# The softmax of a cross-attention on VectorE alone: maximum and sum over the partitions by 32x32 transposes and moves between quadrants

## The chip, the core and the metric

The kernel runs on one core of a Trainium2 chip. The metric is the device time of one execution in microseconds (us). Engines: TensorE (PE) for matrix products, its weight loads listed apart as PEld; VectorE (DVE); ScalarE (ACT); GpSimd (POOL); SyncE (SP), which here only issues transfers.

## What is computed

Everything is float32. `x` has 16 batches of 128 tokens of width 512, `ctx` has 16 batches of 2048 rows of width 512. The reference runs three blocks in order, each on a layer norm of `x`, each added to `x`:

```python
# 1. cross-attention, no projections
scores = einsum('bld,bvd->blv', layernorm(x), ctx)      # 16 x 128 x 2048
x = x + einsum('blv,bvd->bld', softmax(scores, -1), ctx)
# 2. causal self-attention, 16 heads of 32, through 64-wide latents, rotary
#    positions on half of each head
x = x + attention(layernorm(x)) @ Wc
# 3. a mixture of 8 experts of rank 64, two chosen for a batch by its first token
x = x + ffn(layernorm(x))
```

The change lies in the softmax of the first block.

## The kernel before

The program is written out for all 16 batches and three generators are stepped by hand: `score(b)` and `attend(b)` for the cross-attention, `inner(b)` for the self-attention, `experts(b)` for the third block. One pass of the main loop works on four batches at a time: the self-attention of batch b, the rest of the cross-attention (`attend`) of b + 1, the scores of b + 2, and the first norm of b + 3; the experts are those of b - 1.

`score(b)` keeps the scores **transposed**: 128 rows of `ctx` on the partitions, the 128 tokens along the free dimension, so that the exponentials can serve as weights of the next product without being turned. `sc` holds four quarters `v` of [128, 4, 128]. A softmax over the context is then a maximum and a sum over four quarters, over four groups, and over the 128 partitions. Before the change this goes as follows.

- For each quarter TensorE writes `psc`, ACT copies it to `sc`, DVE keeps the running maximum `mx`. `halved` folds four groups to one with two instructions of DVE.
- Over the partitions: TensorE transposes the 128x128 maxima (`tr_m`), DVE reduces each row (`nm`), multiplies the identity with it (`diag`), and TensorE multiplies a matrix of ones with `diag`, which leaves the negated maximum of every token on all partitions (`spread`, in PSUM).
- DVE adds `spread` to the four quarters, ACT takes the exponentials.
- DVE adds the four quarters (`sums`), folds them (`fold`, `last_fold`) to `part`, and in `attend` TensorE multiplies `part` with a column of ones (`den`). DVE takes the reciprocal `rden`, and one instruction, `x<-av,rden,x`, divides and adds the residual.

In the loop these pieces are spread out. The order on TensorE in one pass is: `psc` of b + 2 (with `mid` of the experts inside), `ffn`, `y` of b, `v` of b + 1, `tr_m`, `o` of b, `spread`, then in the next pass `k`, `q`, the first quarter of `av`, the scores of the self-attention (`pss_sc`, `pss_acc`), three more quarters of `av`, `den`, the logits `lg` of the experts, and `psc` again.

Around the change in the same pass, on DVE: the residual of the self-attention (`x<-o,x` of line 687), the norm for the experts (`norm_pieces`: statistics, aggregate, a root on POOL, then `h`), its block transpose (`blocks`, line 268), which SP sends through DRAM to get a full transpose, and the rotary positions for k and q (`rotated`, `turned`): a shuffle, a product with the sines on POOL, a product with the cosines on DVE, and their sum. ACT then makes `kb` out of `kT`. The shuffled k and the shuffled q use one buffer, the tag "partner" with one copy (line 555).

**What sets the order.** Transfers and all of TensorE's instructions are kept in the order in which they are traced. On the other engines a scheduler orders what has no pin, by what it reckons to be ready, and by the order of tracing among those. A pin

```python
def pinned(ins):
    if not closing:
        tc.keep_in_program_order(ins)
```

puts one instruction behind whatever was traced just before it on the same engine, and says nothing about what may come between. In `inner` the shuffles, the cosines and the sums `kT`, `qT` are pinned. The loads of `ctx` and `ctxT` are issued by ACT's queue (`queue = nc.scalar`, line 1049), and `load` pins them too. The end of the last passes is ordered by hand (`CLOSING`). PSUM has three pools: `ps_tr` with 3 banks (`tr_m`, `spread`, `den`, `lg`), `ps_sc` with 2, and `ps_acc` with 3 (`k`, `q`, `av`, `pss_acc`, `mid`, `ffn`, `y`, `v`, `o` in turn).

Of the kernel before, what the change touches and what calls it, by code (L numbers as in the profile page):

```python
# [11 lines left out]
F32 = mybir.dt.float32  # L12
I32 = mybir.dt.int32
U32 = mybir.dt.uint32
AF = mybir.ActivationFunctionType
ALU = mybir.AluOpType
AX = mybir.AxisListType
PSUM = bass.MemoryType.PSUM

P = 128  # L20
B, S, V, D = 16, 128, 2048, 512
# [4 lines left out]
VC = V // 512  # L26
# [4 lines left out]
QD = P // 4  # L31
# [58 lines left out]
def perceiver_block(ctx: ExitStack, tc: tile.TileContext, io: dict, out: bass.AP):  # L90
# [3 lines left out]
    p1 = ctx.enter_context(tc.tile_pool(name="p1", bufs=1))  # L94
    p2 = ctx.enter_context(tc.tile_pool(name="p2", bufs=2))
# [26 lines left out]
    vector, scalar, gpsimd = InOrder(nc.vector), InOrder(nc.scalar), InOrder(nc.gpsimd)  # L122
# [13 lines left out]
    def matmul(*args, **kwargs):  # L136
        tc.keep_in_program_order(nc.tensor.matmul(*args, **kwargs))  # L137
# [11 lines left out]
# [3 lines that stand above are left out]
# [18 lines left out]
    def bank(pool, tag, name):  # L170
        return pool.tile([P, 512], F32, tag=tag, name=name)
# [35 lines left out]
    def layernorm(src, name, mix=False):  # L207
        h, pieces = norm_pieces(src, name, mix=mix)
        for piece in pieces:
            ins = piece()  # L210

            if ins is not None and name.startswith("1_") and piece is not pieces[1]:
                pinned(ins)
        return h
# [46 lines left out]
    def transposed(src, dst, name, by_tensor):  # L261
        n = src.shape[1] // P
        if by_tensor:
            for piece in tensor_pieces(lambda: src, dst, name, n):
                piece()
        else:
            blocks = p1.tile([P, 4, n, QD], F32, tag=f"blocks_{name[0]}", name=f"blocks_{name}")
            vector.transpose(blocks, src.rearrange("p (n q i) -> p q n i", n=n, q=4))
            ways[name] = blocks, dst
# [4 lines left out]
    def named(b, **of):  # L274
        for name, piece in of.items():
            pieces[f"{name}.{b}"] = piece
# [53 lines left out]
    scores, firsts, values, lasts, routes = {}, {}, {}, {}, {}  # L330
# [24 lines left out]
    def first_norm(x, hT):  # L355

        stats = const.tile([P, 6], F32, name="st_first")
        mv, rstd = const.tile([P, 2], F32, name="mv_first"), const.tile([P, 1], F32, name="rs_first")
        vector.bn_stats(stats, x)
        vector.bn_aggr(mv, stats)  # L360
        pinned(gpsimd.tensor_scalar_add(rstd, mv[:, 1:2], EPS))
        gpsimd.tensor_tensor(rstd, rstd, mhalf, ALU.pow)
        h = p2.tile([P, D], F32, tag="h", name="h_1_0")
        for c in range(KC):

            tr = bank(ps_tr, "tr", f"tr_1_0_{c}") if c else bank(ps_acc, "acc", "tr_1_0_0")
            at = slice(c * P, (c + 1) * P)
            vector.tensor_scalar(
                mixed(h)[:, c], plain(x)[:, c], mv[:, 0:1], rstd, ALU.subtract, ALU.mult
            )  # L370
            transpose(tr[:, :P], h[:, at], ident)
            scalar.copy(hT[:, :, c, :], tr[:, :P].rearrange("p (a j) -> p a j", a=4))
            warm_up(1)


    def score(b):

        hT = p1.tile([P, 4, KC, QD], F32, tag="hT1" if b != 1 else "hT3", name=f"hT1_{b}")
        if b:
            h = layernorm(xs[b], f"1_{b}", mix=b == 1)  # L380
            yield
            transposed(h[:], hT, f"1_{b}", b == 1)
        else:
            first_norm(xs[b], hT)
            yield
        yield

        sc = p2.tile([P, VC, 4, S], F32, tag="sc", name=f"sc_{b}")
        mx = p1.tile([P, 4, S], F32, tag="mx", name=f"mx_{b}")
        for v, ct in enumerate(turned_cts.pop(b)):  # L390
            ps = bank(ps_sc, "sc", f"psc_{b}_{v}").rearrange("p (j t) -> p j t", j=4)
            for j in range(4):

                if v == VC - 1 and j == 3:
                    yield
                for c in range(KC):
                    matmul(
                        ps[:, j, :].rearrange("p (a i) -> p a i", a=4),
                        ct[:, c, j * P : (j + 1) * P], hT[:, :, c, :],
                        start=(c == 0), stop=(c == KC - 1),  # L400
                    )
            scalar.copy(sc[:, v], ps)

            if v:
                vector.tensor_tensor(mx, ps, mx if v > 1 else sc[:, 0], ALU.max)
            if v < VC - 1:
                yield

        def halved(t, op):
            vector.tensor_tensor(t[:, :2], t[:, :2], t[:, 2:], op)  # L410
            vector.tensor_tensor(t[:, 0], t[:, 0], t[:, 1], op)
            return t[:, 0]

        most = halved(mx, ALU.max)
        yield

        tr = bank(ps_tr, "tr", f"tr_m_{b}")
        transpose(tr[:, :S], most, ident)
        nm = p2.tile([P, 1], F32, tag="nm", name=f"nm_{b}")
        vector.tensor_reduce(nm, tr[:, :S], AX.X, ALU.max, negate=True)  # L420
        diag = p1.tile([P, S], F32, tag="diag", name=f"diag_{b}")
        vector.tensor_scalar(diag, ident, nm, None, ALU.mult)
        yield
        spread = bank(ps_tr, "tr", f"spread_{b}")
        matmul(spread[:, :S], ones, diag, start=True, stop=True)
        for v in range(VC):
            vector.tensor_tensor(
                sc[:, v], sc[:, v], spread[:, None, :S].to_broadcast([P, 4, S]), ALU.add
            )
            scalar.activation(sc[:, v], sc[:, v], AF.Exp)  # L430
        part = p2.tile([P, S], F32, tag="part", name=f"part_{b}")
        scores[b] = (sc, part)
        yield
        sums = p1.tile([P, 4, S], F32, tag="sums", name=f"sums_{b}")
        pinned(vector.tensor_tensor(sums, sc[:, 0], sc[:, 1], ALU.add))
        yield
        for v in range(2, VC):
            pinned(vector.tensor_tensor(sums, sums, sc[:, v], ALU.add))

        def fold():  # L440
            vector.tensor_tensor(sums[:, :2], sums[:, :2], sums[:, 2:], ALU.add)

        def last_fold():
            vector.tensor_tensor(part, sums[:, 0], sums[:, 1], ALU.add)

        if b == B - 1:
            named(b, fold=fold, last_fold=last_fold)
        else:
            fold()
            last_fold()  # L450
        yield

    def attend(b):

        sc, part = scores.pop(b)
        acc = bank(ps_acc, "acc", f"av_{b}")
        ct = cts.pop(b)

        def quarter(v):
            for j in range(4):  # L460
                matmul(
                    acc, sc[:, v, j, :], ct[v][:, j, :],
                    start=(v == 0 and j == 0), stop=(v == VC - 1 and j == 3),
                )

        state = {}

        def whole():
            den = state["den"] = bank(ps_tr, "tr", f"den_{b}")
            matmul(den[:, :1], part, ones[:, :1], start=True, stop=True)  # L470

        rden = Later(p2, [P, 1], tag="rden", name=f"rden_{b}")

        def inverse():
            vector.reciprocal(rden[:], state["den"][:, :1])

        x1 = Later(p2, [P, D], tag="x1", name=f"x1_{b}")

        def added():
            vector.scalar_tensor_tensor(x1[:], acc, rden[:], xs.pop(b), ALU.mult, ALU.add)  # L480

        if b == B - 1:
            quarter(0)
            named(
                b, av1=lambda: quarter(1), av2=lambda: quarter(2), av3=lambda: quarter(3),
                den=whole, rden=inverse, x1=added,
            )
            h, norm = norm_pieces(x1, f"2_{b}", mix=True)
            named(b, **dict(zip(("st2", "mv2", "rs2", "h2"), norm)))
            firsts[b] = x1, h  # L490
            yield
            return
        for v in range(VC):
            quarter(v)
            if v == (VC - 1 if b else VC - 2):
                whole()
                inverse()
            if v < VC - 1:
                yield
        added()  # L500
        firsts[b] = (x1, layernorm(x1, f"2_{b}", mix=b == 0))
        yield
# [487 lines left out]
    def warm_up(n):  # L990
        for _ in range(n):
            matmul(warm[:, :P], ones, ones, start=True, stop=True)
# [166 lines left out]
```

## Time and profile before

| what | value |
|---|---|
| median of 3 runs | 810.46 us (810.45 to 811.42) |
| profiled execution: its own time | 810.97 us |
| its span in the profile | 809.2 us |
| granted TensorE clock | 0.998 |
| PE busy | 800.2 us (99%) |
| DVE busy | 529.7 us (65%) |
| ACT busy | 260.4 us (32%) |
| POOL busy | 146.6 us (18%) |
| moved by DMA | 211.05 MB, 261 GB/s on average |

Busy times are sums of the durations of an engine's instructions. A group of instructions is given as line, engine, operation, `out<-in`, shape and count; its line is often that of a helper (L137 is the wrapper of every matmul, L115 that of every instruction of DVE, ACT and POOL), so groups are told apart by their tiles. In a timeline the first number is the start from the span's beginning, the second the length of the merged piece, both in us; a bracket at the end gives the idle time before it and what ended it.

### The profile page before, as it was taken

The numbers are of one execution on the slowest core, as the hardware profiler recorded it, in microseconds if no ns is written. First come the engines' busy times: TensorE is split into PE (matmuls) and PEld (weight loads), VectorE is DVE, ScalarE is ACT, GpSimd is POOL, SyncE is SP. The second block draws the span as 40 slices with busy tenths as digits, with TensorE's granted clock in tenths as the row PEclk, the third lists the DMA queues.
The fourth block names the chain that finished last, engine by engine and source line by source line (L and its number), as shares of the span: only waits on it lengthen the run. The fifth ranks groups of instructions, "written<-read, shape, count | busy, mean of one in ns | idle before, by whom it ended". The sixth has DMA issues, their size and how long they took to land.

```text
span 809.2 us, 14363 instructions
## 1 busy us (share of the span) xinstructions
PE 800.2 (99%) x5538; PEld 568.5 (70%) x5538; DVE 529.7 (65%) x1234; ACT 260.4 (32%) x772; POOL 146.6 (18%) x213
## 2 busy tenths in 40 slices
PE   9999999999999999999999999999999999999996
PEld 9946775768677576866758677676867757686653
DVE  2455759386684947658495775938667584856885
ACT  2232324142232423233241232415223241422461
POOL 1001011212121121211112121111212112121204
PEclk9999999999999999999999999999999999999999
DMA  9998394967849497694958859495885949664102
GB/s 375 417 389 321 118 380 171 340 253 251 360 163 381 172 324 292 221 397 142 364 212 292 320 188 399 152 353 222 281 337 181 388 152 340 261 231 173 41 1 79
DMA packets 76868, 211.05 MB, mean 261 GB/s; under 512 B 6400, under 2 KB 42624, under 8 KB 60416
## 3 DMA queue, kind: packets, MB, share of 16 engines
q10 hardware_dynamic: 15696, 113.32, 35.0%
q1 hardware_dynamic: 57168, 84.75, 29.4%
q0 software_dynamic: 3936, 12.07, 4.4%
q8 instruction: 44, 0.72, 0.3%
q14 instruction: 24, 0.20, 0.1%
HBM read 180.23 MB, written 29.88 MB: 260 GB/s over the span
## 4 chain that ended last, share of the span: by engine, by line
PE 97%; DVE 1%; POOL 0%; issue 0%; ACT 0%; POOLq 0%
PE psc L137 28%; PE av L137 28%; PE k L137 7%; PE q L137 7%; PE v L137 7%; PE o L137 6%; PE pss_sc L137 2%; PE y L137 2%; PE ffn L137 2%; PE pss_acc L137 2%; PE mid L137 2%; PE warm L137 1%; PE tr_m L140 0%; PE tr L140 0%; PE spread L137 0%; PE lg L137 0%
## 5 line engine op out<-in xcount | busy, mean ns | idle before, releaser
L137 PE MATMUL psc<-hT,ctxT 128*128 128x128 f32 x2048 | 235.0, 276 | 0.0
L137 PEld LDWEIGHTS psc<-hT,ctxT 128*128 128x128 f32 x2048 | 231.3, 192 | 0.5 <-issue 0.5
L137 PE MATMUL av<-ctx,sc 128*128 128x512 f32 x512 | 227.3, 596 | 0.0
L137 PEld LDWEIGHTS av<-ctx,sc 128*128 128x128 f32 x512 | 94.4, 190 | 110.5 <-issue 107.9
L115 ACT ACTIVATE att<-att,nmx 128x128 f32<-128x128 f32 x256 | 98.8, 388 | 84.9 <-DVE nmx L115 84.9
L115 POOL TENSOR_SCALAR rs<-mv 128x1 f32<-128x1 f32 x47 | 10.6, 225 | 431.0 <-DVE g_at L115 209.5
L115 ACT COPY sc<-psc 128x512 f32<-128x512 f32 x64 | 37.5, 586 | 140.0 <-PE psc L137 140.0
L115 ACT ACTIVATE sc<-sc 128x512 f32<-128x512 f32 x64 | 40.2, 630 | 90.9 <-DVE sc L115 90.4
L137 PE MATMUL k<-hT,w_k 128*128 128x128 f32 x512 | 60.1, 275 | 0.0
L137 PE MATMUL q<-hT,w_q 128*128 128x128 f32 x512 | 60.0, 275 | 0.0
L137 PEld LDWEIGHTS k<-hT,w_k 128*128 128x128 f32 x512 | 58.5, 192 | 1.5 <-issue 0.8
L137 PE MATMUL v<-w_v,hT 128*32 128x512 f32 x520 | 59.0, 593 | 0.0
L137 PEld LDWEIGHTS q<-hT,w_q 128*128 128x128 f32 x512 | 58.5, 192 | 0.0
L137 PE MATMUL o<-w_c,yT 128*128 128x512 f32 x128 | 57.8, 594 | 0.0
L115 DVE TENSOR_TENSOR mx<-psc,mx 128x512 f32<-128x512 f32 x32 | 21.6, 676 | 55.0 <-ACT sc L115 55.0
L115 ACT ACTIVATE kb<-kT,cst 128x512 f32<-128x512 f32 (+1 forms) x34 | 36.2, 1113 | 39.8 <-DVE kT L115 39.8
L115 DVE TENSOR_SCALAR h<-x,mv,rs 128x512 f32<-128x512 f32 x47 | 27.4, 583 | 31.9 <-POOL rs L115 31.9
L115 ACT ACTIVATION_READ_ACCUMULATOR att<-att,nmx 128x1 f32 x256 | 47.9, 187 | 0.0
L115 DVE TENSOR_TENSOR sc<-sc,spread 128x512 f32<-128x512 f32 x64 | 42.6, 671 | 3.3 <-PE spread L137 3.3
L115 DVE TENSOR_TENSOR att<-att,rsm 128x512 f32<-128x512 f32 x64 | 43.4, 678 | 0.8
L115 DVE TENSOR_REDUCE nmx<-att 128x4 f32<-128x512 f32 x64 | 41.8, 671 | 0.1
L137 PEld LDWEIGHTS o<-w_c,yT 128*128 128x128 f32 x128 | 23.9, 196 | 23.8 <-issue 23.0
(139 smaller groups left out, 851.1 us busy)
## 6 DMA issues: line engine op xcount, KB each, us to landing
ctx<-in_ctx_dram ACTq DMA_DIRECT2D x56, 1024.0 KB, 8.4
ctxT<-in_ctxT_dram ACTq DMA_DIRECT2D x52, 1024.0 KB, 10.5
there_p<-pX SPq DMA_DIRECT2D x28, 512.0 KB, 4.0
pT<-there_p SPq DMA_DIRECT2D x28, 512.0 KB, 4.5
ctxT<-in_ctxT_dram SPq DMA_DIRECT2D x12, 1024.0 KB, 8.9
there<-blocks SPq DMA_DIRECT2D x42, 256.0 KB, 3.3
hT<-there SPq DMA_DIRECT2D x42, 256.0 KB, 3.0
ctx<-in_ctx_dram SPq DMA_DIRECT2D x8, 1024.0 KB, 10.5
```

The lines of the kernel that those rows point to most:

```text
L115: ins = issue(*args, **kwargs)
L137: tc.keep_in_program_order(nc.tensor.matmul(*args, **kwargs))
```

## The change

For batches 2 to 15 the maximum over the partitions stays on DVE. A new helper `across` transposes the 128x128 tile in blocks of 32x32, reduces along the free dimension to four values a partition, moves three quadrants of 32 partitions beside the first, and reduces again: partition i of the first quadrant then holds the values of tokens i, 32 + i, 64 + i and 96 + i. For the maximum four more block transposes of a broadcast write the result into all four quadrants, as `spread` in SBUF. The four subtractions follow at once, behind the last scores, and the first two exponentials with them; the last two exponentials and the first of the `sums` are traced one step later (behind the loads of the next `ctxT`), the other two `sums` another step later. Batches 2 to 14 take the denominator by `across` as well, with a reciprocal and four moves, and `attend` finds it ready, without `den`. Batches 0 and 1 keep the old way, and batch 15 keeps the old denominator, its `sums` where they were.

```diff
+    def across(t, name, op, negate=False):
+        turned = p1.tile([P, 4, QD], F32, tag="diag", name=f"turned_{name}")
+        pinned(vector.transpose(turned.rearrange("p q i -> p (q i)"), t))
+        each = p2.tile([P, 4, 4], F32, tag="each_quadrant", name=f"each_quadrant_{name}")
+        pinned(vector.tensor_reduce(each[:, 0, :], turned, AX.X, op))
+        for a in range(1, 4):
+            pinned(vector.tensor_copy(each[:QD, a, :], each[a * QD : (a + 1) * QD, 0, :]))
+        whole = p2.tile([P, 4], F32, tag="whole", name=f"whole_{name}")
+        pinned(vector.tensor_reduce(
+            whole[:QD], each[:QD].rearrange("p a q -> p q a"), AX.X, op, negate=negate
+        ))
+        return whole[:QD]
...
         most = halved(mx, ALU.max)
+        if b > 1:
+            spread = p1.tile([P, 4, QD], F32, tag="spread", name=f"spread_{b}")
+            peak = across(most, f"m_{b}", ALU.max, negate=True)
+            for a in range(4):
+                pinned(vector.transpose(
+                    spread[a * QD : (a + 1) * QD], peak[:, :, None].to_broadcast([QD, 4, QD])
+                ))
+            for v in range(VC):
+                pinned(vector.tensor_tensor(
+                    sc[:, v], sc[:, v],
+                    spread.rearrange("p j i -> p (j i)")[:, None, :].to_broadcast([P, 4, S]), ALU.add,
+                ))
+                if v < 2:
+                    scalar.activation(sc[:, v], sc[:, v], AF.Exp)
+            yield
+            for v in range(2, VC):
+                pinned(scalar.activation(sc[:, v], sc[:, v], AF.Exp))
+            sums = p1.tile([P, 4, S], F32, tag="sums", name=f"sums_{b}")
+            if b == B - 1:
...
+            pinned(vector.tensor_tensor(sums, sc[:, 0], sc[:, 1], ALU.add))
+            yield
+            for v in range(2, VC):
+                pinned(vector.tensor_tensor(sums, sums, sc[:, v], ALU.add))
+            yield
+            whole = across(halved(sums, ALU.add), f"den_{b}", ALU.add)
+            vector.reciprocal(whole, whole)
+            rden = p2.tile([P, 1], F32, tag="rden", name=f"rden_{b}")
+            for a in range(4):
+                vector.tensor_copy(rden[a * QD : (a + 1) * QD], whole[:, a : a + 1])
+            scores[b] = (sc, rden)
+            yield
+            yield
+            return
         yield
 
         tr = bank(ps_tr, "tr", f"tr_m_{b}")
...
-        rden = Later(p2, [P, 1], tag="rden", name=f"rden_{b}")
+        known = 1 < b < B - 1
+        rden = part if known else Later(p2, [P, 1], tag="rden", name=f"rden_{b}")
...
-            if v == (VC - 1 if b else VC - 2):
+            if not known and v == (VC - 1 if b else VC - 2):
                 whole()
                 inverse()
```

More of the change, by code (lines that the diff above doesn't have):

```diff
@@ L414, in score @@
         most = halved(mx, ALU.max)
+        if b > 1:
[17 more added lines that the diff above has]
+            if b == B - 1:
+                part = p2.tile([P, S], F32, tag="part", name=f"part_{b}")
+                scores[b] = (sc, part)
+                yield
[4 more added lines that the diff above has]
+                    pinned(vector.tensor_tensor(sums, sums, sc[:, v], ALU.add))
+                named(
+                    b, fold=lambda: vector.tensor_tensor(sums[:, :2], sums[:, :2], sums[:, 2:], ALU.add),
+                    last_fold=lambda: vector.tensor_tensor(part, sums[:, 0], sums[:, 1], ALU.add),
+                )
+                yield
+                return
+            pinned(vector.tensor_tensor(sums, sc[:, 0], sc[:, 1], ALU.add))
+            yield
+            for v in range(2, VC):
+                pinned(vector.tensor_tensor(sums, sums, sc[:, v], ALU.add))
+            yield
+            whole = across(halved(sums, ALU.add), f"den_{b}", ALU.add)
[4 more added lines that the diff above has]
+            scores[b] = (sc, rden)
+            yield
+            yield
+            return
         yield
@@ L444, in last_fold @@
             vector.tensor_tensor(part, sums[:, 0], sums[:, 1], ALU.add)
[L446 to L450, printed above, removed]
+        fold()
+        last_fold()
         yield
```

## The prediction

> **What bounds the kernel now.** I read the page first: the busy rows, then the chain that ended last. Both say TensorE (PE).
>
> ```profile
> span 809.2 us, 14363 instructions
> PE 800.2 (99%) x5538; PEld 568.5 (70%) x5538; DVE 529.7 (65%) x1234; ACT 260.4 (32%) x772; POOL 146.6 (18%) x213
> ...
> PE 97%; DVE 1%; POOL 0%; issue 0%; ACT 0%; POOLq 0%
> ```
>
> PE has almost no idle time; VectorE (DVE) has a third of the span free. So only what leaves PE, or makes PE wait, can move the time. The groups show what the change takes from PE: `tr_m` (16 records of 322 ns), `spread` (32 of 276 ns), `den` (32 of 208 ns). [...]the price on PE is the distance between starts. The timeline of PE over one steady iteration gives it; the other iterations repeat these distances every 47.86 us.
>
> ```profile
> 394.18 3.62 PE L137 MATMUL v<-w_v,hT 128*32 128x512 f32 x32
> 397.72 0.33 PE L140 MATMUL tr_m<-ident,mx 128*128 128x128 f32 x1
> 397.89 3.60 PE L137 MATMUL o<-w_c,yT 128*128 128x512 f32 x8
> 401.32 0.39 PE L137 MATMUL spread<-diag,ones 128*128 128x128 f32 x2
> 401.55 3.74 PE L137 MATMUL k<-hT,w_k 128*128 128x128 f32 x32
> 405.12 3.74 PE L137 MATMUL q<-hT,w_q 128*128 128x128 f32 x32
> 408.69 3.60 PE L137 MATMUL av<-ctx,sc 128*128 128x512 f32 x8
> 412.22 1.13 PE L137 MATMUL pss_sc<-kb,qT 64*128 64x256 f32 x8
> ...
> 424.55 0.28 PE L137 MATMUL den<-ones,part 128*128 128x1 f32 x2
> 424.69 0.37 PE L137 MATMUL lg<-g_part,ones 128*128 128x8 f32 x2
> ```
>
> The reader sees that `tr_m` holds PE for 0.17 us (397.72 to 397.89), `spread` for 0.23, `den` for 0.14. Then the timeline of DVE over the same stretch, to see what could make PE wait once these are gone:
>
> ```profile
> 398.42 0.29 DVE L115 TENSOR_SCALAR diag<-ident,nm 128x128 f32<-128x128 f32 x1
> 401.53 0.69 DVE L115 TENSOR_TENSOR x<-o,x 128x512 f32<-128x512 f32 x1 [2.82 <-PE o L137]
> 402.13 0.68 DVE L115 TENSOR_TENSOR sc<-sc,spread 128x512 f32<-128x512 f32 x1
> ...
> 405.10 0.55 DVE L115 TENSOR_SCALAR h<-x,mv,rs 128x512 f32<-128x512 f32 x1 [0.43 <-POOL rs L115]
> 405.56 0.68 DVE L115 TENSOR_TENSOR sc<-sc,spread 128x512 f32<-128x512 f32 x1
> 406.17 0.01 DVE L115 LOAD_MASK_SELECT kP<-k  x1
> 406.17 0.73 DVE L115 STREAM_SHUFFLE kP<-k 128x512 f32<-128x512 f32 x1
> ...
> 408.29 0.69 DVE L115 TENSOR_TENSOR kT<-kT,kP 128x512 f32<-128x512 f32 x1 [0.20 <-POOL kP L115]
> ...
> 411.31 0.69 DVE L115 TENSOR_TENSOR qT<-qT,qP 128x512 f32<-128x512 f32 x1 [0.89 <-POOL qP L115]
> ```
>
> This is the reading that decides. `qT` ends at 412.00 and `pss_sc`, which reads it, starts at 412.22; where PE waits for DVE in the closing it starts 0.05 us after DVE's end (`h` 762.81, `tr` 762.86), so the slack is 0.17 us. And from the k shuffle on the chain is rigid: shuffle, POOL's product with the sines (1.28 us), `kT`, then the q shuffle, which must wait because `kP` and `qP` share one buffer ("partner"), POOL again, `qT`. From shuffle k (406.17) to the end of `qT` it takes 5.83 us. Shuffle k itself was late because of DVE: k was through on PE at 405.12, and 0.21 us later DVE could have had it (the distance at 72.08 to 72.29, where DVE did wait for k); but it was busy until 406.17. So whatever DVE does between `x<-o,x` (called x2 below) and shuffle k already sits 0.17 us under the critical path.
>
> **The change part by part.**
>
> *Removed from PE*, for batches 2 to 15 `tr_m` and `spread`, for 2 to 14 `den`. `tr_m` is worth less than 0.17: the first matmul behind the 32-column v products shows its weight load uncovered (`tr_m` and its load both start at 397.72; the first av behind `pss_acc` lasts 0.70 against 0.59), and o inherits that 0.11. So 0.06 to 0.17; I take 0.10. With `spread` 0.23 and `den` 0.14 an iteration gains up to 0.47 us if nothing waits.
>
> *The maximum on DVE.* Removed: `nm` 0.29, `diag` 0.29. Added, none of it in the trace in this shape, so from the nearest rows: a block transpose of 128x128 (transposes of 512 columns 0.70, a slope of 1.04 ns a column from the 512, 256 and 128-column TENSOR_TENSOR rows: 0.30), a reduce to four (0.29, `nm`), three moves between quadrants (`g_z` copy 0.14), a reduce of 16 (`g_part` 0.18), four transposes of 32 partitions (0.30 each at most, 0.22 if they overlap like other independent instructions), eight dependent starts at 0.04. Sum 2.3 to 2.8 us. Then four subtractions at 0.60 from start to start (both inputs in SBUF; `sums`, both in SBUF, has 0.69 against 0.67, so the same), and the first sum 0.70. It starts when the second halving ends (394.6) and includes `res<-ffn` (0.6) between: ended at 400.6 to 401.1. DVE was idle there (2.9 us before `nm`, 2.8 us before x2), and x2 cannot start before o ends at 401.36. So this costs nothing while it is under 6.7 us; each 0.1 us beyond goes onto the path.
>
> [...]independent instructions of 0.68 start 0.60 apart. [...] No row of this trace has a quadrant change[...]. [...]by this trace PE pays about 0.10 and DVE over 2 us, and that is harmless only because DVE idles here.
>
> *The sums moved forward.* Before, four subtractions lay between x2 and shuffle k, and three of them filled waits of the norm chain (x2, statistics, POOL's root, `h`). Now they are gone from there, but the second and third `sums` come in, and both are pinned behind the last thing traced on DVE, which is this `h`; shuffle k is pinned behind them. They can't fill the norm's waits. And the unpinned transpose of `h` into `blocks` (0.70) is ready 0.58 after `h`, while `sums` waits for exponentials that stand behind four `ctxT` issues on ACT (1.95 us, 397.94 on); so I expect the scheduler to put it ahead. From x2: statistics +0.73, aggregate +0.72, `h` +1.18 (403.92 to 405.10), `blocks` +0.58, `sums` +0.64 (transpose to next, 388.20 to 388.84), `sums` +0.80 (dependent: two took 1.49), shuffle k +0.61. Sum 5.26, against 4.64 before (401.53 to 406.17).
>
> *The denominator.* Halving and the reduction over partitions (2 to 2.5 us of DVE) take the place of three `sums` and two folds (3.0 us, 411.92 to 414.98). They lie behind `qT`, or, being unpinned at their head, in the two waits for POOL (0.89 each). Two halvings take 0.75 and fit; a third instruction would overrun by 0.17, and small ones in the second wait by up to 0.1. I take 0.05 in all, 0.3 as the bound. Behind `qT` they cost nothing: the masks came at 414.90 with `pss_sc` done at 413.4, and will come earlier. The new reciprocal and four moves replace one reciprocal; only `x<-av` waits for them, 12 us later.
>
> *ACT and queues.* The first two exponentials now stand ahead of v's copy and the four `ctxT` issues, about 1.3 us; those loads land within some 12 us and are used at 424.9, 25 us on. v's bank is wanted by q at 405, the copy is through by 400. SP's and POOL's queues keep their order. Cover is ample.
>
> *The sum for one iteration,* counted from o's end (401.32 before). PE alone would reach `pss_sc` at 10.90 - 0.23 = 10.67. DVE: x2 at 0.21, shuffle k at 5.47, end of `qT` at 11.30, PE at 11.35, with the overrun 11.40. Before: 10.90. So +0.50, less `tr_m` 0.10 and `den` 0.14: +0.26 us. It holds for the 13 iterations in which batches 2 to 14 have their sums there: +3.4. The last one has none there and keeps its gain of 0.33. Together +3.1. The profiled execution took 810.97 (span 809.2 and 1.8 around it), 0.5 above the median of 810.46; its differences go onto the median: 813.5.
>
> **The rivals.**
>
> *Faster: DVE keeps up.* If `blocks` stays behind shuffle k as it does now, h to shuffle is 0.46 + 0.80 + 0.61 = 1.87 instead of 2.63, `pss_sc` could start at 10.64, and PE is the bound again: 13 x 0.47 + 0.33 = 6.4 us less, 804.0. For it: PE at 99%, and today's order has `blocks` behind `kT<-k`. Against: `blocks` stood back there because ready work stood before it, and pinned `sums` is not ready as early. If it slips between the two sums, into the dependent wait, 0.32 is saved: -0.06 an iteration, 809.4.
>
> *Slower by much: the first sum is late too.* If the scheduler puts the first two exponentials behind the `ctxT` issues, the first `sums` also falls between `h` and shuffle k: 0.7 more an iteration, +9.1, 822.6. The same price falls due if the maximum's chain exceeds 6.7 us by that much. For it: four `ctxT` issues did stand ahead of every exponential; against: the first subtraction should end near 398.5, when v's copy has only begun.
>
> *Slower by a bank.* The accumulators have three banks in rotation, so o takes the bank of ffn, freed by `res<-ffn` on DVE (394.54). Were that queued behind the subtractions, to 400.4, o would start 2.7 us late: over 30 us in all, 845. Against: it is ready at 393.4, before the new chain starts, and each dependent step leaves room.
>
> *The work doesn't leave PE* in batches 0 and 1; elsewhere nothing of the old path is left, so I give this nothing.
>
> **How the numbers follow.** `blocks` ahead (forecast) 0.52, own range 811 to 817 from the bounds of `tr_m`, overrun and margin; between the sums 0.16; PE-bound 0.12; late first sum 0.15; bank 0.05. The range 804 to 823 takes in all but the bank and the tails. A measurement can tell 0.2% (1.6 us) here: under 808.8 counts as faster: the PE-bound case, a third of the 809.4 case, a tail of the forecast: 0.20. Over 812.1: 0.60. Between: 0.20.
>
> **What would show it.** Right: PE rows without `tr_m`, iterations of about 48.1 us, an idle of about 0.7 us on PE or its weight load before `pss_sc`, put down to `qT` or `kb`; DVE in the order h, blocks, sums, sums, shuffle k; shuffle k over 5 us behind x2. Wrong: iterations of 47.4 us and no such idle (first rival); idle of PE before o (bank); x2 starting more than 0.3 us behind o's end, which would mean that the quadrant instructions cost more than their bound.

## The result: 0.6% slower, through one wait in every iteration

The changed kernel takes 816.34 us (median of 6 runs, 814.8 to 816.88). The kernel before took 810.9 in its 6 runs beside it. The ratio is 1.0063, with a 95% interval of 1.0051 to 1.0074. (Medians and ranges here and below are of all executions, while a ratio leaves out one that lies over 1.5% above the kernel's fastest, as there is in experiments 7, 10 and 11, so it isn't the quotient of two medians.) The forecast was +3.1 us; measured are +5.4. The profiled execution is the shortest of the six: 814.8 us, with a span of 813.0.

First the page of the kernel after: the busy rows, then the engines' shares of the chain that ended last.

```profile
span 813.0 us, 14443 instructions
PE 792.6 (97%) x5470; PEld 562.3 (69%) x5470; DVE 591.6 (73%) x1476; ACT 259.7 (32%) x772; POOL 146.4 (18%) x213
...
PE 78%; DVE 13%; POOL 4%; issue 3%; DMA 1%; POOLq 0%; ACT 0%; DVEq 0%
```

PE has lost 7.6 us of work (800.2 before) and is busy for a smaller share of a longer span. DVE has gained 61.9 us of work. The chain was 97% PE and is now 78% PE; DVE and POOL hold 17% of it. So PE waits for them somewhere. The view of waits on PE of the kernel after names the place; its columns are the total, the number of times and the longest.

```profile
PE pss_sc L137 <- DVE qT L115: 11.1, 13, 1.3
```

Before, no wait of `pss_sc` was among PE's waits. Now there is one in each of 13 iterations. The timeline of PE over one iteration of the kernel after shows its size.

```profile
379.64 0.28 PE L137 MATMUL lg<-g_part,ones 128*128 128x8 f32 x2
...
400.44 3.70 PE L137 MATMUL o<-w_c,yT 128*128 128x512 f32 x8
403.98 3.73 PE L137 MATMUL k<-hT,w_k 128*128 128x128 f32 x32
407.55 3.74 PE L137 MATMUL q<-hT,w_q 128*128 128x128 f32 x32
411.13 3.60 PE L137 MATMUL av<-ctx,sc 128*128 128x512 f32 x8
415.54 1.13 PE L137 MATMUL pss_sc<-kb,qT 64*128 64x256 f32 x8 [0.81 <-DVE qT L115]
...
427.87 0.28 PE L137 MATMUL lg<-g_part,ones 128*128 128x8 f32 x2
```

`tr_m`, `spread` and `den` are gone. In exchange `pss_sc` stands 4.41 us behind the start of `av` (411.13 to 415.54) where it stood 3.53 behind it before (408.69 to 412.22). From `lg` to the next `lg` (379.64 to 427.87) an iteration takes 48.23 us, against 47.86 before: +0.37, where +0.26 was forecast.

The timeline of DVE over the same iteration of the kernel after tells why `qT` is late.

```profile
397.38 0.31 DVE L115 STREAM_TRANSPOSE turned_m<-mx 128x128 f32<-128x128 f32 x1
...
398.64 0.50 DVE L115 COPY each_quadrant_m<-each_quadrant_m 32x4 f32<-32x4 f32 x3
...
399.38 1.25 DVE L115 STREAM_TRANSPOSE spread<-whole_m 32x128 f32<-32x128 f32 x4
400.66 2.50 DVE L115 TENSOR_TENSOR sc<-sc,spread 128x512 f32<-128x512 f32 x4
403.08 0.69 DVE L115 TENSOR_TENSOR sums<-sc 128x512 f32<-128x512 f32 x1
404.18 0.69 DVE L115 TENSOR_TENSOR x<-o,x 128x512 f32<-128x512 f32 x1 [0.42 <-PE o L137]
...
406.83 0.55 DVE L115 TENSOR_SCALAR h<-x,mv,rs 128x512 f32<-128x512 f32 x1 [1.01 <-POOL rs L115]
407.41 0.71 DVE L115 STREAM_TRANSPOSE blocks<-h 128x512 f32<-128x512 f32 x1
408.04 1.45 DVE L115 TENSOR_TENSOR sums<-sums,sc 128x512 f32<-128x512 f32 x2
...
409.41 0.73 DVE L115 STREAM_SHUFFLE kP<-k 128x512 f32<-128x512 f32 x1
...
410.63 1.14 DVE L115 TENSOR_TENSOR sums<-sums 128x256 f32<-128x256 f32 x1
411.69 0.68 DVE L115 TENSOR_TENSOR kT<-kT,kP 128x512 f32<-128x512 f32 x1
...
414.70 0.69 DVE L115 TENSOR_TENSOR qT<-qT,qP 128x512 f32<-128x512 f32 x1 [0.67 <-POOL qP L115]
...
417.21 0.69 DVE L115 TENSOR_TENSOR att<-pss_sc,cst 128x512 f32<-128x512 f32 x1
```

Upper half: the maximum's chain with four subtractions and the first sum runs from 397.38 to 403.77, and DVE still idles 0.42 us before x2 (`x<-o,x`). It costs nothing. Lower half: between `h` and shuffle k stand `blocks` and two `sums`, and shuffle k starts 5.23 us behind x2, against 4.64 before.

### The profile page after: what moved, and what is told of

The parts are those of the page before. It is cut to its first block, busy times and chain, and to the rows that moved or that the text cites. A ratio compares the mean times of both kernels' runs of the same rounds, so it can differ in the third digit from the quotient of the medians.

```text
span 813.0 us, 14443 instructions
## 1 busy us (share of the span) xinstructions
PE 792.6 (97%) x5470; PEld 562.3 (69%) x5470; DVE 591.6 (73%) x1476; ACT 259.7 (32%) x772; POOL 146.4 (18%) x213
## 4 chain that ended last, share of the span: by engine, by line
PE 78%; DVE 13%; POOL 4%; issue 3%; DMA 1%; POOLq 0%; ACT 0%; DVEq 0%
PE psc L137 28%; PE av L137 22%; PE v L137 7%; PE o L137 7%; DVE sums L115 2%; PE pss_sc L137 2%; POOL qP L115 2%; DVE kT L115 2%; PE y L137 2%; PE pss_acc L137 2%; PE mid L137 2%; PE ffn L137 2%; POOL rs L115 1%; PE k L137 1%; PE q L137 1%
## 5 line engine op out<-in xcount | busy, mean ns | idle before, releaser
L115 ACT ACTIVATE sc<-sc 128x512 f32<-128x512 f32 x64 | 38.2, 627 | 70.5 <-DVE sc L115 55.9
L115 DVE TENSOR_TENSOR mx<-psc,sc 128x512 f32<-128x512 f32 x16 | 11.0, 690 | 47.7 <-ACT sc L115 47.7
```

Of the source, the lines that this page charges most:

```text
L115: ins = issue(*args, **kwargs)
```

## The experiments

The kernel before, run beside these kernels on the same chips, has medians of 810.55 to 810.95 us. Three places for the loss were to be told apart: the order `blocks`, `sums`, `sums` in front of shuffle k; the denominator on DVE itself; the rigid stretch behind shuffle k.

### 1. The two sums back behind qT

```diff
+            yield
+            yield
             pinned(vector.tensor_tensor(sums, sc[:, 0], sc[:, 1], ALU.add))
             yield
             for v in range(2, VC):
                 pinned(vector.tensor_tensor(sums, sums, sc[:, v], ALU.add))
-            yield
             whole = across(halved(sums, ALU.add), f"den_{b}", ALU.add)
...
             scores[b] = (sc, rden)
-            yield
             yield
             return
```

> The changed kernel with the three sums of a batch back behind qT, where they stood before the change; maximum, subtractions, exponentials and the reduction for the denominator stay on VectorE. Theory (the sums in front of shuffle k, pinned behind the norm, are what makes PE wait for qT): x2 to shuffle k falls from 5.23 to about 3.85 us, PE no longer waits before pss_sc, an iteration is 47.4 us, and the time is 6 us below before, near 804.5. Rival (more DVE work as such, 62 us of it, is too much for the engine): some wait stays or moves to the self-attention's softmax behind pss_sc, and the time is not below before.

Measured: 815.31 us (814.98 to 815.9), ratio 1.0056 (1.0043 to 1.0069). The wait at `pss_sc` is gone and the time is not. Waits on PE, and PE's timeline, of this kernel:

```profile
PE lg L137 <- DVE g_part L115: 7.9, 12, 0.7
```

```profile
414.11 1.14 PE L137 MATMUL pss_sc<-kb,qT 64*128 64x256 f32 x8
...
427.26 0.39 PE L137 MATMUL lg<-g_part,ones 128*128 128x8 f32 x2 [0.66 <-DVE g_part L115]
```

PE now waits later in the pass, for the router's sums, which DVE makes behind the masks and the softmax of the self-attention. DVE's timeline of this kernel shows the queue:

```profile
414.38 1.49 DVE L115 TENSOR_TENSOR sums<-sums,sc 128x512 f32<-128x512 f32 x2
...
418.18 0.65 DVE L115 TENSOR_TENSOR att<-pss_sc,cst 128x512 f32<-128x512 f32 x1
...
427.02 0.18 DVE L115 TENSOR_REDUCE g_part<-g_share 128x8 f32<-128x32 f32 x1
```

The first mask starts 4.07 us behind `pss_sc`, because sums and reduction now both stand between `qT` and it; in the kernel after it starts 1.67 behind (417.21 against 415.54). So the forecast of 804.5 for this edit failed, and its rival came true: the early wait was exchanged for a late one.

### 2. The maximum alone

For all batches from 2 on, the branch that only batch 15 takes in the change: new maximum, sums behind `qT`, folds, `den` on TensorE.

```diff
-            if b == B - 1:
+            if True:
...
-        known = 1 < b < B - 1
+        known = False
```

> Only the maximum on VectorE (with the subtractions at once); sums, folds and the matmul for the denominator as before the change. Theory: shuffle k is early, PE bound, the 14 batches gain 0.33 us each for tr_m and spread: 4.6 us below before, near 806. Rival (the maximum's chain with its quadrant moves is what costs): no gain or a loss.

Measured: 806.83 us (805.83 to 807.05), ratio 0.9952 (0.9939 to 0.9965), as expected. No new wait. Timeline of DVE, then of PE:

```profile
399.85 0.69 DVE L115 TENSOR_TENSOR x<-o,x 128x512 f32<-128x512 f32 x1 [1.02 <-PE o L137]
...
403.72 0.73 DVE L115 STREAM_SHUFFLE kP<-k 128x512 f32<-128x512 f32 x1
```

```profile
375.22 0.37 PE L137 MATMUL lg<-g_part,ones 128*128 128x8 f32 x2
...
422.79 0.37 PE L137 MATMUL lg<-g_part,ones 128*128 128x8 f32 x2
```

Shuffle k stands 3.87 us behind x2, and the iteration takes 47.57 us: 0.29 less than before. Of that `spread` was 0.23, so `tr_m` was worth 0.06, the lower end of its range.

### 3. The denominator alone

The old maximum for every batch; `across(halved(sums))` behind the sums in the old place.

```diff
-        if b > 1:
+        if False:
...
+        known = 1 < b < B - 1
...
-        fold()
-        last_fold()
+        if known:
+            whole = across(halved(sums, ALU.add), f"den_{b}", ALU.add)
+            vector.reciprocal(whole, whole)
...
+            scores[b] = (sc, rden)
```

> Only the denominator on VectorE; maximum, spread and subtractions as before the change, the sums behind qT as before. Theory: the chain up to qT is untouched, 13 batches gain the 0.14 us of den: about 1.8 us below before, near 809. Rival (reduction and moves delay the softmax of the self-attention until y waits): slower than before.

Measured: 833.32 us (825.36 to 836.87), ratio 1.0248 (1.0206 to 1.0291): far slower than expected. Waits on PE of this kernel:

```profile
PE lg L137 <- DVE g_part L115: 14.4, 13, 1.2
PE v L137 <- DMA hT<-there: 3.9, 1, 3.9
```

It is the wait of experiment 1, larger: the first masks start 5.06 us behind `pss_sc` (424.52 against 419.46), and an iteration takes 49.07 us. So the reduction of the denominator is the dear part of the change when it stands behind the sums. Where the sums have left that place (the kernel after and experiments 4 to 6, 9 and 12), no such wait of `lg` is among PE's waits.

### 4. The experts' block transpose pinned

```diff
-            vector.transpose(blocks, src.rearrange("p (n q i) -> p q n i", n=n, q=4))
+            turn = vector.transpose(blocks, src.rearrange("p (n q i) -> p q n i", n=n, q=4))
+            if name[0] == "3":
+                pinned(turn)
```

> The changed kernel with one pin more: the block transpose of the norm for the experts is kept behind the cosines of k, so it cannot stand between the norm and the sums. Theory: shuffle k comes 0.63 us earlier (0.58 + 0.64 for the transpose and its dependence less 0.46 for a step that is now independent, about 0.75 at most), so the wait of 0.82 us before pss_sc falls to 0.1 to 0.2; 13 iterations x 0.63 = 8 us below the changed kernel, near 807.5 to 808. Rival (the sums alone, not what stands before them, set the wait; or the wait is for kb): under 2 us below the changed kernel.

Measured: 807.37 us (806.63 to 807.43), ratio 0.9955 (0.9942 to 0.9967), as expected. Timeline of DVE of this kernel:

```profile
401.22 0.69 DVE L115 TENSOR_TENSOR x<-o,x 128x512 f32<-128x512 f32 x1 [0.42 <-PE o L137]
...
404.32 1.48 DVE L115 TENSOR_TENSOR sums<-sums,sc 128x512 f32<-128x512 f32 x2
405.73 0.73 DVE L115 STREAM_SHUFFLE kP<-k 128x512 f32<-128x512 f32 x1
...
406.94 0.70 DVE L115 STREAM_TRANSPOSE blocks<-h 128x512 f32<-128x512 f32 x1
...
410.01 1.08 DVE L115 TENSOR_TENSOR sums<-sums 128x128 f32<-128x128 f32 x1
```

With `blocks` behind shuffle k, shuffle k stands 4.51 us behind x2 (401.22), PE waits for `qT` once in the whole run (0.9 us), and the iteration is 47.52 us. One pin takes the change from slower to faster: the 0.72 us by which it shortens the way from x2 to shuffle k (5.23 less 4.51) undo the loss. In this order `blocks` also fills POOL's wait in front of `kT`, which keeps the first halving of the sums out of it; experiment 5 tells these two effects apart.

### 5 and 6. The halvings pinned behind qT, without and with pin 4

```diff
-            whole = across(halved(sums, ALU.add), f"den_{b}", ALU.add)
+            pinned(vector.tensor_tensor(sums[:, :2], sums[:, :2], sums[:, 2:], ALU.add))
+            pinned(vector.tensor_tensor(sums[:, 0], sums[:, 0], sums[:, 1], ALU.add))
+            whole = across(sums[:, 0], f"den_{b}", ALU.add)
```

> The changed kernel with the two halvings of the sums pinned behind qT, so that none runs while POOL multiplies the shuffled k with the sines. In the changed kernel the first halving takes 1.15 us there instead of 0.42 and ends 0.16 us after POOL. Theory (two inputs from SBUF beside POOL's product wait for it): both halvings take 0.42 and 0.29 again, kT comes 0.17 us earlier, and so does pss_sc: 13 x 0.17 = 2.2 us below the changed kernel, near 814. Rival (the length of that row is a flaw of the record, or the wait is set elsewhere): within 0.5 us of the changed kernel.

> Both pins: block transpose behind the cosines of k, halvings behind qT. Theory: 0.63 + 0.17 us off a wait of 0.82, so PE hardly waits any more; 10.4 us below the changed kernel at most, near 805.5 to 806.5, though the sums still stand in front of shuffle k. Rival: the two overlap, and the second pin adds nothing to the first (807.5 to 808).

Measured: 813.93 us (813.79 to 814.29), ratio 1.0040 (1.0027 to 1.0053) for the halvings alone; 805.63 us (804.76 to 809.66), ratio 0.9943 (0.9926 to 0.9960) with both pins. Both as expected. The groups of instructions by shape, first of the kernel after, then of the kernel with the halvings pinned (total, mean ns of one, idle before):

```profile
L115 DVE TENSOR_TENSOR sums<-sums 128x256 f32<-128x256 f32 x16 | 16.2, 1015 | 0.1
```

```profile
L115 DVE TENSOR_TENSOR sums<-sums 128x256 f32<-128x256 f32 x16 | 6.7, 419 | 0.1
```

The same addition takes 419 ns alone and mostly 1.14 us when it fell beside POOL's product. (It ends 0.28 us behind POOL's product in the kernel after, not 0.16 as the expectation has it.) Without the second pin the wait at `pss_sc` shrank from 0.82 to 0.65 us and the iteration from 48.24 to 48.07, which is what was expected of it.

### 7. The last quarter's sum one step later

```diff
-            for v in range(2, VC):
-                pinned(vector.tensor_tensor(sums, sums, sc[:, v], ALU.add))
+            pinned(vector.tensor_tensor(sums, sums, sc[:, 2], ALU.add))
             yield
+            pinned(vector.tensor_tensor(sums, sums, sc[:, 3], ALU.add))
             whole = across(halved(sums, ALU.add), f"den_{b}", ALU.add)
```

> The changed kernel with one of the two sums (the last quarter) traced one step later, behind qT; the other stays in front of shuffle k. A dose: theory, x2 to shuffle k shrinks by that one instruction with its dependence, 0.73 to 0.80 us, and the wait of 0.82 us nearly goes (the halvings leave POOL's wait too, 0.17): near 805.5 to 806.5, as far down as both pins. Rival (a fixed delay by the pin behind the norm, however many sums follow it): the wait stays over 0.5 us, 812 or more.

Measured: 820.18 us (815.26 to 831.88), ratio 1.0088 (1.0065 to 1.0111). It was expected near 806. Half of the expectation held: the wait at `pss_sc` shrank to 0.3 us once, and an ordinary iteration takes 47.35 us. But three passes were hit by something else. PE's waits and timeline of this kernel:

```profile
PE v L137 <- DMA hT<-there: 10.3, 3, 3.9
```

```profile
541.98 5.34 PE L137 MATMUL v<-w_v,hT 128*32 128x512 f32 x32 [3.85 <-DMA hT<-there]
```

`hT` is the turned norm that v reads, brought back from DRAM by SP. The DMA issues of this kernel, over the whole run and in the window of 520 to 545 us (KB each, median us from issue to landing):

```profile
hT<-there SPq DMA_DIRECT2D x42, 256.0 KB, 2.9
```

```profile
hT<-there SPq DMA_DIRECT2D x1, 256.0 KB, 10.2
```

With one more addition ahead of it, DVE reaches the next norm later, and the transfer is issued later: 21.8 to 23.3 us behind `pss_sc` in the passes behind the first, against 20.0 to 20.6 in the kernel after. The three passes that were hit are those with the latest issues, 22.7, 23.0 and 23.3. The one shown here fell under the loads of `ctx`: from 535 to 542 us the DMA engines moved 418 GB/s at a busy share of 1.02. That the loads stretched it is a reading of this window; no run here takes the loads away.

### 8. The kernel before with one addition more

An unused addition of 128x512 is pinned in front of shuffle k, to measure what room the kernel before had there.

```diff
+            if n == "k" and chunks == every:
+                extra = p1.tile([P, 512], F32, tag="mx", name=f"extra_{b}")
+                pinned(vector.tensor_tensor(extra, cst[:, :512], cst[:, :512], ALU.add))
```

> The kernel before, unchanged but for one addition of 128x512 on VectorE (its result is used by nobody) pinned directly in front of shuffle k in 14 iterations. Theory (before the change that place already lay 0.07 to 0.17 us under the critical path): shuffle k comes 0.61 us later, pss_sc 0.45 to 0.54 us: 6.3 to 7.5 us slower than before, near 817.5 to 818. Rival (DVE has 35% of the span free, so half a microsecond is absorbed): within 1.6 us of before.

Measured: 818.45 us (818.05 to 819.76), ratio 1.0100 (1.0085 to 1.0114): 7.5 us slower, at the upper end of what was expected. Timeline of DVE, then waits on PE of this kernel:

```profile
409.23 0.69 DVE L115 TENSOR_TENSOR extra<-cst 128x512 f32<-128x512 f32 x1
```

```profile
PE pss_sc L137 <- DVE qT L115: 6.4, 14, 0.5
```

The iteration is 0.53 us longer (48.39) for 0.61 us added: the kernel before had 0.08 us of room there. The mechanism is shown without any part of the change: of what was added between x2 and shuffle k, all but 0.08 us was paid.

### 9. The shuffled q in a buffer of its own

```diff
-            tag = "partner" if n == "k" or chunks == every else "blocks_3"
+            tag = "mx" if n == "q" and chunks == every else "partner" if n == "k" else "blocks_3"
```

> The changed kernel with the shuffled q in a buffer of its own (the maxima's, free at that time), so that its shuffle need not wait until kT has read the shuffled k. Theory (from shuffle k to qT the chain is rigid, one of its links being the shared buffer, 0.81 from kT to shuffle q against 0.61 for independent instructions): qT 0.2 us earlier in 13 iterations, 2.6 us below the changed kernel, near 813.7. Rival (shuffle q waits for q on PE or for something else): no difference from the changed kernel.

Measured: 812.22 us (811.21 to 813.68), ratio 1.0020 (1.0011 to 1.0029). By the medians it gave 4.1 us where 2.6 were expected. Shuffle q starts 0.61 us behind `kT` instead of 0.81, so the shared buffer cost 0.20 an iteration. The wait at `pss_sc` is 0.56 us in an ordinary iteration, and the iteration takes 47.98 us, 0.26 less than in the kernel after: 3.4 us in 13. Where the other 0.06 an iteration and the rest of the medians' difference come from isn't placed.

### 10 and 11. The denominator later still

Halvings and reduction are traced where `den` stood, behind the softmax: once with the sums of experiment 1, once with the pin of experiment 4.

```diff
-            whole = across(halved(sums, ALU.add), f"den_{b}", ALU.add)
...
+            def den():
+                pinned(vector.tensor_tensor(sums[:, :2], sums[:, :2], sums[:, 2:], ALU.add))
+                pinned(vector.tensor_tensor(sums[:, 0], sums[:, 0], sums[:, 1], ALU.add))
+                whole = across(sums[:, 0], f"den_{b}", ALU.add)
...
+            scores[b] = (sc, den)
...
+            if known and v == VC - 1:
+                rden = part()
```

> The kernel with the sums back behind qT, and the halvings and the reduction for the denominator traced where den stood, behind three quarters of the self-attention's softmax. Theory (with the sums back it was the 2.4 us of reduction ahead of the masks that made lg wait 0.66 us for the router's share on VectorE's queue): lg no longer waits, 13 x 0.66 = 8.6 us below the kernel with the sums back, near 806.5, against about 3 us more if the later x1 makes v wait for its turned input. Rival (the work must be done in this stretch wherever it stands): about 815 as with the sums back.

> The kernel with the block transpose pinned behind the cosines of k (sums in front of shuffle k as in the changed kernel), and halvings and reduction for the denominator moved to where den stood. Theory: no halving beside POOL's product (0.17), so pss_sc waits no more than 0.05, and the masks come 2 us earlier: PE bound, 804.5 to 806. Rival: x1 comes 2 us later behind the reduction, its turned input arrives late, and v waits in some iterations: over 808.

Measured: 822.22 us (813.73 to 832.44), ratio 1.0123 (1.0080 to 1.0166), and 817.67 us (811.75 to 830.54), ratio 1.0070 (1.0042 to 1.0099). Both miss their forecasts of 806.5 and 804.5 to 806; the second's rival, that v waits, came true. The first lost its wait at `lg`, as expected, and was slower than experiment 1 all the same. Waits on PE of the one and of the other:

```profile
PE v L137 <- DMA hT<-there: 6.9, 2, 4.2
```

```profile
PE v L137 <- DMA hT<-there: 12.5, 3, 8.0
```

The wait of experiment 7 again. Most iterations take 47.34 to 47.55 us in both, as fast as in experiment 12 or nearly so, and the time is mostly lost in the few passes in which `hT` is late: the longest takes 53.46 us in the one and 58.0 in the other. The times spread by over 18 us within each kernel; that these passes make the spread is likely but not shown, since one execution of each was traced. So the reduction has no safe place behind the softmax either: the norm whose transfer v waits for comes next.

### 12. Both pins and the buffer

The edits of 4, 5 and 9 together:

```diff
+                pinned(turn)
...
+            pinned(vector.tensor_tensor(sums[:, :2], sums[:, :2], sums[:, 2:], ALU.add))
+            pinned(vector.tensor_tensor(sums[:, 0], sums[:, 0], sums[:, 1], ALU.add))
+            whole = across(sums[:, 0], f"den_{b}", ALU.add)
...
+            tag = "mx" if n == "q" and chunks == every else "partner" if n == "k" else "blocks_3"
```

> Both pins (block transpose behind the cosines of k, halvings behind qT) and a buffer of its own for the shuffled q; the whole computation of the changed kernel. Theory: qT has 0.2 us to spare in every iteration, PE waits nowhere before pss_sc, an iteration is 47.4 us, 6 us below before, near 804.8, and no turned input is late. Rival: nothing left to gain over both pins (805.6), since their wait was already gone.

Measured: 805.1 us (804.29 to 805.16), ratio 0.9925 (0.9912 to 0.9939) to the kernel before, whose median was 810.55. It is faster than both kernels. The page of this kernel, then its waits on PE and PE's timeline:

```profile
PE 793.9 (99%) x5470; PEld 562.4 (70%) x5470; DVE 586.1 (73%) x1476; ACT 259.9 (32%) x772; POOL 146.5 (18%) x213
...
PE 96%; DVE 2%; POOL 1%; issue 0%; ACT 0%; POOLq 0%; DVEq 0%
```

```profile
PE pss_sc L137 <- DVE qT L115: 0.5, 1, 0.5
```

```profile
374.92 0.28 PE L137 MATMUL lg<-g_part,ones 128*128 128x8 f32 x2
...
422.27 0.28 PE L137 MATMUL lg<-g_part,ones 128*128 128x8 f32 x2
```

PE is the bound again, with the work of the three products gone: an iteration takes 47.35 us, 0.51 less than before. DVE carries as many instructions as in the kernel after (1476). Their order, and one buffer, made the difference.

## Why the prediction held

**The mechanism** was the one forecast. The range of 804 to 823 was wide enough to take in the first rival too, so the time alone says little; the rows and the experiments decide: `blocks` was drawn ahead of the two pinned `sums`, both stood in front of shuffle k, and the rigid stretch behind shuffle k carried the delay to `pss_sc`. Experiment 4 shows it by taking away one of the three, and experiment 8 by adding one to the kernel before. The first rival (DVE keeps up) priced the order with `blocks` behind shuffle k at 804.0, and experiments 4 and 12, which make that order, measure 807.37 and 805.1.

**The steps from x2 to shuffle k** were summed to 5.26 us and measured 5.23 (404.18 to 409.41). The maximum's chain was put at 6.0 to 6.5 us from the end of the halving and took 6.43 (397.34 to 403.77). It left DVE 0.42 us of idle time before x2, where the prediction's upper end leaves 0.26 (401.10 to 401.36). (The 401.36 that the prediction gives there as the end of o is the start of x2, 401.53, less the 0.17 of `tr_m`.)

**The instructions that change the quadrant** were priced on the author's assumption that none overlaps the next, which no row of the trace before shows: the 0.5 us between 400.6 and 401.1 in the prediction. (An estimate from its rows is 0.56: independent instructions of 0.68 start 0.60 apart, and seven overlaps of 0.08 are lost.) It came out so. Three moves between quadrants take 0.50 us at 158 ns each, four transposes of 32 partitions 1.25 us at 302 ns each: none overlaps the next. The four independent subtractions that follow, 0.69 us each, take 2.50 together and do overlap. No run here tests the reason. The price was hidden by the idle time before x2, as forecast.

**The step that was mis-sized** is the overrun of the halvings, put at 0.05 us. It said that two halvings of 0.75 together fit into POOL's wait of 0.89. The first one did not fit: it starts at 410.63, while POOL works on the sines' product, and takes 1.14 us instead of 0.42.

```profile
410.22 1.27 POOL L115 TENSOR_TENSOR kP<-kP,cst 128x512 f32<-128x512 f32 x1 [3.43 <-DVE kP L115]
```

POOL ends at 411.49 and the halving at 411.77, 0.28 us later. In experiment 4 the halving of 128 columns falls beside POOL's product for q and ends 0.15 us behind it (411.09 against 410.94). At the 1.04 ns a column of the prediction, 256 columns are 0.27 us and 128 are 0.13: by this estimate nearly all the columns ran behind POOL's end. From shuffle k to `kT` it takes 2.28 us, against 2.12 before: 0.16 lost. The second halving, 0.28 us, fell into the gap that the shared buffer leaves in front of shuffle q and cost nothing. This stretch of the trace before could not show it: beside POOL's two products (406.98 to 408.26, 410.00 to 411.28) it has no addition with both inputs in SBUF. `blocks`, which filled this wait before, has one input and took its 0.69 us (407.39). Experiment 5 shows the difference, 1015 ns in the mean against 419; why the halving is long beside POOL and short elsewhere isn't shown.

**The other terms.** From `qT`'s end to PE it took 0.15 us (415.39 to 415.54) instead of 0.05. With it, the slack of 0.17 us that the prediction gave the kernel before is 0.07, which fits the 0.08 of experiment 8. From o's end to `pss_sc` that makes 11.56 us for a forecast 11.40. PE's gain was 0.06 for `tr_m` (forecast 0.10) and 0.22 for `den` (forecast 0.14; from experiment 2 to experiment 12, 47.57 to 47.35), with `spread` 0.51 for all three where 0.47 was forecast. So 0.66 more less 0.28: +0.38, and measured +0.37.

**The sum over the run.** At the `pss_sc` of batch 14 the two traces lie 5.08 us apart: the first of the 13 iterations loses 1.04 (its wait is 1.28 us, which isn't placed), twelve lose 0.38 each, and the last step, without sums, gives 0.51 back. The closing of the profiled execution gives 1.3 us back, so the spans differ by 3.8 and the medians by 5.4. Where the five longer executions lose 0.5 to 2 us more stays open; none of them was traced.

**One claim stood on less than it said:** that the denominator costs nothing behind `qT`. It is true in the changed kernel, where its masks start 1.67 us behind `pss_sc`. Experiments 1 and 3 show that it is true only because the sums were moved forward: with the sums and the reduction both there, PE waits 0.66 to 1.17 us for `g_part`. Moved behind the softmax (experiments 10 and 11), the reduction makes v wait in some passes. Of the orders tried, the one of experiment 12 works best: sums in front, `blocks` and the halvings held back.

## What to carry to other kernels

When work moves from a bound engine to one with a third of its time free, ask in which stretch that third lies: add up the engine's order between two fixed points of the path, as from x2 to shuffle k here, and measure the room with one unused instruction pinned in front. When some instructions of a stretch are pinned, look at what the scheduler may still draw ahead of them; one more pin was worth 9 us here (experiment 4). A wait for another engine is cover only for work that can run while that engine does: in POOL's wait `blocks` took its 0.69 us, and the first halving 1.14 instead of 0.42.

## What was not expected of the hardware

- A 128x256 addition on VectorE with both inputs in SBUF took 1.14 us beside a 1.27 us product on GpSimd, ending 0.28 behind it, against 0.42 alone; a 128x128 one took 1.08 (experiment 4) against 0.29. A transpose, with one input, was not stretched: `blocks` took 0.70 us within POOL's product (experiment 4, 406.94 against POOL's 406.53 to 407.81) and 0.71 away from it (the kernel after, 407.41).
- After 3.85 us without work, TensorE took 5.34 us for the v products that take 3.62 without a wait. The windows view of experiment 7 shows it; behind the stretch and its length come the busy times of five engines with their counts, then the granted clock (0.76), the DMA share and the GB/s:

```profile
541.00:548.00 7.00, 6.02 (x34) 2.07 (x35) 4.16 (x9) 1.80 (x3) 0.05 (x1) 0.76 0.65 263
```

- The transfer of 256 KB from DRAM takes 2.9 us in the median and took 10.2 us in a window with 418 GB/s.
- A wait can cost PE more than the idle time that the profile gives: in experiment 1 a wait of 0.66 us in front of `lg` moved it by 0.82 (`av` to `lg` 11.23 us instead of 10.41), and the `lg` behind it took 0.10 longer to the next product.
